# Two groups per scan in a Mamba layer: moving the decay factors from PSUM to SBUF, with smaller edits around it and in the last layer

## The chip, the core and the metric

The kernel runs on one core of a Trainium2 chip. A core has five engines with an instruction queue each: TensorE (PE) for matrix products, VectorE (DVE), ScalarE (ACT) and GpSimd (POOL) for elementwise work, and SyncE (SP), which here issues the DMA transfers. Operands lie in SBUF or, for results of PE, in the eight banks of PSUM. POOL here works on SBUF only. The metric is the device time of the whole kernel in microseconds (us): a single launch that computes all four layers. Before the change it is 8328.65 us, the median of three runs (8322.74 to 8329.06).

## The reference

The input is four images of 56 x 56 positions with 128 channels, in fp32. Four layers follow, each added to its input: a neighbourhood attention, a Mamba block, an additive attention with a mixture of 64 experts, and a full attention with 8 experts of which each token takes two. The change touches the second and the last.

The Mamba layer runs two passes over 224 sequences (4 images x 56 rows) of 56 steps. In each, 256 inner channels have 16 states each:

```python
delta = jax.nn.softplus(dt @ dtw + dtb)
A = -jnp.exp(A_log)
deltaA  = exp(delta[.., d] * A[d, n])           # decay of a state
deltaBu = delta[.., d] * u[.., d] * Bm[.., n]   # its input
h = deltaA * h + deltaBu                        # along the 56 steps
y = sum over n of h * Cm[.., n];   y = y + u * Dp
```

The last layer's experts work on a layer norm of the tokens, x:

```python
router_probs = softmax(x @ router_w + router_b)     # 8 experts
top_p, top_i = top_k(router_probs, 2);  top_p = top_p / sum(top_p)
expert_out = einsum('bnd,edc->bnec', x, expert_w) + expert_b
out = sum over the two of top_p * expert_out
```

## The kernel before, in words

The kernel works through the layers one after the other. Within a layer the order of instructions on PE, ACT, DVE and POOL is written out by hand: each engine runs its own instructions in the order in which the Python code emits them, and waits at an instruction until what it needs is there.

**Layer 1 (Mamba), `layer1`.** Tokens are cut into 28 chunks of 448 (8 sequences of 56). A chunk and one of the two passes make a block; there are 56 blocks (`order`). A block's 256 x 16 states are taken 128 at a time as 32 groups: 8 channels with 16 states each fill the 128 partitions, and the 448 tokens lie along the row. Two groups are a pair, so a block has 16 pairs (`PAIRS`) and the layer 896 (`n_pairs`). For each pair p the main loop emits:

- `select(p + 1)`: PE spreads delta times A over the 128 states (matrix "A_pick", tile "a", L650) and delta times u (matrix "pick", tile "u", L657), two matmuls each of 32 input rows. ACT turns "a" into the decay exp(a), in place, in PSUM (L660). "a" has two buffers of two banks, "u" one of two banks, "y" and the general tile "m" one bank each: PSUM is full.
- `scan(p)`: DVE runs the recurrence along the row, one scan for each of the two groups (L672). At a sequence's first step delta is set to 1e30, so that the decay is 0 and the scan starts afresh. POOL multiplies the result by C (tile "bc", L676), in place.
- `sums(p - 5)`, at every second pair: PE adds the 16 states of a channel into "y" (L682). The states "hs" have seven buffers.
- `inputs(p + 1)`: DVE multiplies "u" by B into "dBu", one product for each group (L667).

Around the pairs, `first` and `last` place the other steps of a block at fixed pairs. `mamba_pre` prepares the next block during the present one: a convolution by PE ("raw"), silu on ACT, a projection, spreads of delta, B and C by PE (L808), the softplus, whose maximum with 0 is on DVE (`parts`, L818) and whose last three steps are on POOL (L834, L837, L840), and "du" = delta times u in two halves of 64 partitions each on POOL (L846), with rows exchanged so that the four matmuls of a pair lie on four different sets of 32 rows. `gate` (L697, DVE), `project` (PE) and `pass_on` finish a block.

**Layer 3, `layer3`.** For each image and chunk of 448 queries, 25 key tiles are worked off as units: `weights` makes scores "q" on PE (L1548) and their exponent on ACT, `weighted` adds up "o" on PE (L1559), which has a single bank. Other steps stand at fixed units in `at`: `prepare_chunk` of the next image, `experts_chunk` of the last chunk (copy of "o", L1533 and L1534, then the return to tokens, and `token_choice`: a layer norm, the router with its bias added by DVE, the choice of two, the biases of the experts by a transposed gate and a matmul, L1706 to L1720, then the experts themselves, L1726 and L1731). During the first chunks the experts of layer 2 for the last image run between these units, with a PSUM bank of their own ("h").

**Layer 0** matters for reading the profile: its weights "e" are multiplied by a table (L428), three heads on DVE and one on POOL, with all operands in SBUF.

Of the kernel before, what the change touches and what calls it, by code (L numbers as in the profile page):

```python
# [10 lines left out]
AF = mybir.ActivationFunctionType  # L11
ALU = mybir.AluOpType
# [7 lines left out]
P = 128  # L20
# [17 lines left out]
PAIRS = DI // 16  # L38
LONG = 1.0e30

AH = 16
# [63 lines left out]
class Hybrid:  # L105
# [485 lines left out]
    def layer1(self):  # L591
# [5 lines left out]
        with ExitStack() as ctx:  # L597
# [20 lines left out]
            h = {}  # L618
            pre, yg, A, U, V, HS, py = {}, {}, {}, {}, {}, {}, {}

# [15 lines left out]
            def place(p):  # L636

                j, i = divmod(p, PAIRS)
                return j, i // 8, i // 2 % 4, i % 2 * 2

            def select(p):
                if p >= n_pairs:
                    return
                j, f, q, r0 = place(p)
                l = order[j][2]
                A[p] = self.t(ps_a, [P, 2, 512], "a")[:, :, :CH]
                U[p] = self.t(ps_u, [P, 2, 512], "u")[:, :, :CH]
                for k in range(2):
                    own = slice((r0 + k) * HD, (r0 + k + 1) * HD)
                    nc.tensor.matmul(  # L650
                        A[p][:, k], w["A"][own, l, f, q, :], pre[j]["delta"][own, f],
                        start=True, stop=True,
                    )
                for k in range(2):
                    r = (r0 + k + 2) % 4
                    own = slice(r * HD, (r + 1) * HD)
                    nc.tensor.matmul(  # L657
                        U[p][:, k], w["pick"][own, q, :], pre[j]["du"][own, f], start=True, stop=True
                    )
                nc.scalar.activation(A[p], A[p], AF.Exp)  # L660

            def inputs(p):
                if p < n_pairs:
                    V[p] = self.t(sm, [P, 2, CH], "dBu")
                    u = U.pop(p)
                    for k in range(2):
                        nc.vector.tensor_mul(V[p][:, k], u[:, k], pre[p // PAIRS]["bc"][:, 0])  # L667

            def scan(p):
                HS[p] = self.t(sm, [P, 2, CH], "hs", bufs=7)  # L670
                for k in range(2):
                    nc.vector.tensor_tensor_scan(  # L672
                        HS[p][:, k], A[p][:, k], V[p][:, k], 0.0, op0=ALU.mult, op1=ALU.add
                    )
                bc = pre[p // PAIRS]["bc"]
                nc.gpsimd.tensor_mul(HS[p], HS[p], bc[:, 1:2].to_broadcast([P, 2, CH]))  # L676
# [76 lines left out]
            for p in range(-PAIRS - 2, n_pairs + PAIRS):  # L753
                for step in first.get(p, []):
                    step()
                if p >= -1:
                    select(p + 1)
                if 0 <= p < n_pairs:
                    scan(p)
                if p % 2 and 0 <= p - 5 < n_pairs:  # L760
                    sums(p - 5)
                for step in last.get(p, []):
                    step()
                if p >= -1:
                    inputs(p + 1)

    def mamba_pre(self, pre, j, block, h, w, sm, m):
# [44 lines left out]
        def parts(i):  # L812
            if i == 0:
                r["e"] = self.t(sm, [P, NHALF, CH], "sp_e", bufs=1)
                r["delta"] = self.t(sm, [P, NHALF, CH], "delta")
            dtb = w["dtb"][:, l, i : i + 1]
            nc.scalar.activation(r["e"][:, i], ps[0], AF.Abs, bias=dtb)
            nc.vector.tensor_scalar(r["delta"][:, i], ps[0], dtb, 0.0, op0=ALU.add, op1=ALU.max)  # L818

# [21 lines left out]

        def du(k):
            if k == 0:
                r["du"] = self.t(sm, [P, NHALF, CH], "du")
            to, of = slice(k * 64, k * 64 + 64), slice(64 - k * 64, 128 - k * 64)
            nc.gpsimd.tensor_mul(r["du"][to], r["delta"][of], r["us"][of])  # L846
            if k == 1:

                for f in range(NHALF):
                    nc.gpsimd.memset(seqs(r["delta"][:, f])[:, :, 0:1], LONG)  # L850

# [7 lines left out]
        def resed(f):  # L859
# [11 lines left out]
            (6, spread, 2), (7, low), (7, spread, 3), (8, log1p), (9, delta), (9, res, 0),  # L871
            (10, du, 0), (10, res, 1), (11, du, 1), (PAIRS + 2, silu, "raw_res", "sres"),
        ]
# [588 lines left out]
    def layer3(self):  # L1462
# [6 lines left out]
        with ExitStack() as ctx:  # L1469
            wp = ctx.enter_context(tc.tile_pool(name="l3_w", bufs=1))  # L1470
            w = {}
            w["rw"] = self.load(wp, [P, E3], "rw", a["L3_ffn_router_w"])
            w["rb"] = self.load(wp, [TP, E3], "rb", a["L3_ffn_router_b"].partition_broadcast(TP))
            w["ew"] = self.load(wp, [P, E3, C], "ew", a["L3_ffn_expert_w"].rearrange("e d c -> d e c"))
            w["eb"] = self.load(wp, [E3, C], "eb", a["L3_ffn_expert_b"])
            shift = self.t(wp, [P, 1], "shift")
# [9 lines left out]
            ps_m = ctx.enter_context(tc.tile_pool(name="l3_m", bufs=2, space=PSUM))  # L1486
            ps_h = ctx.enter_context(tc.tile_pool(name="l3_h", bufs=1, space=PSUM))
            ps_e = ctx.enter_context(tc.tile_pool(name="l3_e", bufs=2, space=PSUM))
            ctx.enter_context(
                tc.manual_schedule(engines={ET.PE, ET.Activation, ET.DVE, ET.Pool})  # L1490
# [64 lines left out]
            def weighted(b, c, t):  # L1555
                if t == 0:
                    po[b, c] = self.t(ps_o, [P, 512], "o")[:, :CH]
                n = tiles[t][1]
                nc.tensor.matmul(  # L1559
                    po[b, c], xk[b][:n, t, :], es.pop((b, c, t))[:n], start=(t == 0), stop=(t == N - 1)  # L1560
                )
# [26 lines left out]
            for steps, num in ((chosen, 4), (passed, 2)):  # L1588
                for n, step in enumerate(steps):
                    at.setdefault(u // den, []).append(step)  # L1590
                    u += 0 if step.holds else num
            assert u // den < 2 * NCH * N + 6
            for u in range(max(at) + 3):
                if u < len(units):
                    weights(*units[u])
                if 0 <= u - 2 < len(units):
                    weighted(*units[u - 2])
                for step in at.get(u - 2, []):
                    step()
# [8 lines left out]

    def normed_chunk(self, b, c, sm, m, eps, turned):

# [21 lines left out]
        def norm():  # L1632
            r["xa"] = self.t(sm, [TP, TC, C], "lc_xa", bufs=4)
            for k in range(TC):
                nc.vector.tensor_scalar(
                    r["xa"][:, k, :], x[:, TC * c + k, :], r["mv"][:, k, 0:1], r["r"][:, k : k + 1],
                    op0=ALU.subtract, op1=ALU.mult,
                )

        def turn():  # L1640
# [10 lines left out]
    def token_choice(self, b, c, w, sm, m, ps_e):  # L1651
# [11 lines left out]
        def route():  # L1663
            ps = m()
            for k in range(TC):
                nc.tensor.matmul(
                    ps[:TP, k * E3 : (k + 1) * E3], r["xT"][:, k * TP : (k + 1) * TP], w["rw"],
                    start=True, stop=True,
                )


            r["pr"] = pr = tile4("r_pr", 2 * E3 - K3)
            nc.gpsimd.memset(pr[:, :, E3:], NOTHING)
            r["p8"] = p8 = pr[:, :, 0:E3]
            nc.vector.tensor_tensor(
                p8, ps[:TP, : TC * E3].rearrange("p (t e) -> p t e", e=E3),
                w["rb"].unsqueeze(1).to_broadcast([TP, TC, E3]), op=ALU.add,
            )
            r["red"] = red = self.t(sm, [TP, TC], "r_red")
            nc.vector.tensor_reduce(red, p8, axis=AX.X, op=ALU.max)  # L1680
            nc.vector.tensor_tensor(p8, p8, per_token(red), op=ALU.subtract)

# [19 lines left out]

        def turn_gate():
            r["pg"] = pg = m()
            for k in range(TC):
                nc.tensor.transpose(  # L1706
                    pg[:E3, k * TP : (k + 1) * TP], r["gate"][:, k, :], self.ident[:TP, :TP]
                )

        def turned_gate():  # L1710
            r["gT"] = self.t(sm, [E3, CH], "gT")
            nc.scalar.copy(r["gT"], r["pg"][:E3, :CH])

        def biases():
            pb = m().rearrange("p (k c) -> p k c", c=C)
            for k in range(TC):
                nc.tensor.matmul(
                    pb[:TP, k, :], r["gT"][:, k * TP : (k + 1) * TP], w["eb"], start=True, stop=True
                )
            nc.vector.tensor_add(x4, pb[:TP], x4)  # L1720

        def experts(k):
# [13 lines left out]
        def store():  # L1736
# [4 lines left out]
        return (  # L1741
            self.normed_chunk(b, c, sm, m, w["eps"], turned)
            + [(10, route), (12, exp), (13, choose), (18, turn_gate), (19, turned_gate), (21, biases)]
            + [(21 + 2 * k, bind(experts, k)) for k in range(TC)] + [(21 + 2 * TC, store)]
# [44 lines left out]
```

## Time and profile before

| what | value |
|---|---|
| median of three runs | 8328.65 us |
| the profiled execution | 8338.93 us, its span 8337.2 us |
| busy PE, DVE, ACT, POOL | 84%, 75%, 61%, 35% of the span |
| Mamba (645 to 3825 us of the span) | 3180 us, 56 blocks |
| layer 3 (from 6720 us) | 1617 us |
| granted clock of PE in the span | 0.924 |

The profile page and the trace come from the same execution. In a line of groups there stand the source line, the engine, the operation, output and inputs by the program's names, the shapes and the count; then the total busy time in us and the mean of one in ns; then the idle time of the engine just before these instructions, and who ended most of it. [...] consecutive instructions can overlap a little in the records, and an instruction that has been started and then has to wait inside the engine shows a longer time.

### The profile page before, as it was taken

What the parts mean: (1) busy time and instruction counts of PE and PEld (TensorE: products, weight loads), DVE (VectorE), ACT (ScalarE), POOL (GpSimd) and SP (SyncE); (2) the same over time, 40 slices, a digit from 0 to 9 for tenths busy, and PEclk for the clock granted to TensorE, in tenths of its full rate; (3) what the DMA queues carried; (4) which work ended last, traced back from release to release, by engine and by line L of the source; (5) the groups of instructions that cost most, each with busy time, mean ns of one, the idle gap of its engine ahead of it and who ended that gap; (6) DMA issues with size and microseconds to landing.
All of it is one profiled execution on the core that took longest, in us unless ns stands there. A gap on an engine that the chain in (4) does not pass through costs nothing.

```text
span 8337.2 us, 109252 instructions
## 1 busy us (share of the span) xinstructions
PE 7035.0 (84%) x41373; PEld 2773.9 (33%) x41373; DVE 6274.1 (75%) x12303; ACT 5125.5 (61%) x5001; POOL 2902.1 (35%) x1997
## 2 busy tenths in 40 slices
PE   8878998999899999996777777777777889999998
PEld 4432333333333332332222222222222344454444
DVE  6768998999898899897777878777787754344434
ACT  4445555555455555554998799889889964333332
POOL 4537876877677768772000000000001000000000
PEclk9988998999898889897999999999999989999999
DMA  2000000000000000000000000000003101210000
GB/s 51 1 13 1 1 1 1 1 1 1 1 1 1 1 1 1 1 1 5 1 1 1 5 1 1 1 5 1 1 25 113 44 4 54 86 44 5 5 5 6
DMA packets 84469, 102.05 MB, mean 12 GB/s; under 512 B 21132, under 2 KB 49700, under 8 KB 83236
## 3 DMA queue, kind: packets, MB, share of 16 engines
q1 hardware_dynamic: 83941, 95.06, 3.8%
q8 instruction: 327, 5.36, 0.3%
q14 instruction: 201, 1.64, 0.1%
HBM read 84.76 MB, written 10.29 MB: 11 GB/s over the span
## 4 chain that ended last, share of the span: by engine, by line
PE 48%; ACT 21%; DVE 20%; issue 9%; POOL 1%; SPq 0%; ACTq 0%; DMA 0%; DVEq 0%; POOLq 0%
ACT th L1021 12%; DVE hs L672 7%; PE q L1548 6%; PE o L1559 6%; PE a L650 6%; PE s L1032 5%; PE m L779 5%; DVE th L1012 5%; PE y L682 3%; PE o L1059 2%; PE pe L1726 2%; PE u L657 2%; DVE e L428 2%; DVE dBu L667 2%; PE m L808 1%
## 5 line engine op out<-in xcount | busy, mean ns | idle before, releaser
L1021 ACT ACTIVATE th<-th 128x3136 f32<-128x3136 f32 (+12 forms) x1120 | 2293.3, 2094 | 217.6 <-DVE th L1012 169.2
L1012 DVE TENSOR_SCALAR th<-fT,g 128x784 f32<-128x784 f32 (+6 forms) x3920 | 1934.3, 561 | 468.2 <-PE s L1032 440.5
L676 POOL TENSOR_TENSOR hs<-hs,bc 128x896 f32<-128x896 f32 x896 | 1859.0, 2084 | 688.8 <-DVE hs L672 578.3
L1032 PE MATMUL s<-th,place 128*32 128x392 f32 (+7 forms) x14336 | 1487.7, 491 | 714.5 <-ACT th L1021 711.1
L672 DVE TENSOR_TENSOR_SCAN hs<-a,dBu 128x448 f32<-128x448 f32 x1792 | 1845.1, 1070 | 160.8 <-POOL hs L676 87.4
L660 ACT ACTIVATE a<-a 128x896 f32<-128x896 f32 x896 | 808.5, 902 | 931.2 <-PE u L657 431.0
L650 PE MATMUL a<-delta,A_pick 32*128 32x448 f32 x3584 | 1080.3, 638 | 97.0 <-DVE hs L672 93.1
L657 PE MATMUL u<-du,pick 32*128 32x448 f32 x3584 | 1033.8, 656 | 26.7 <-DVE dBu L667 22.6
L667 DVE TENSOR_TENSOR dBu<-u,bc 128x448 f32<-128x448 f32 x1792 | 1014.1, 606 | 45.8 <-PE u L657 40.8
L1032 PEld LDWEIGHTS s<-th,place 128*32 128x32 f32 (+1 forms) x14336 | 423.0, 111 | 1648.8 <-ACT th L1021 1130.5
L1553 ACT ACTIVATE e<-q,shift 128x448 f32<-128x448 f32 (+1 forms) x700 | 443.0, 634 | 774.3 <-PE q L1548 774.0
L1559 PE MATMUL o<-e,xk 128*128 128x448 f32 (+1 forms) x1400 | 657.3, 551 | 61.4 <-ACT oT L1534 61.4
L1548 PE MATMUL q<-xT 128*128 128x448 f32 (+1 forms) x1400 | 656.1, 551 | 7.7 <-ACT e L1553 7.7
L1050 POOL TENSOR_TENSOR e<-e,later 112x112 f32<-112x112 f32 x112 | 79.6, 710 | 1589.8 <-ACT e L1043 961.9
L650 PEld LDWEIGHTS a<-delta,A_pick 32*128 32x128 f32 x3584 | 338.3, 202 | 706.8 <-issue 327.5
L682 PE MATMUL y<-hs,sum 128*32 128x448 f32 x3584 | 494.4, 626 | 3.6 <-POOL hs L676 3.6
L1731 DVE SCALAR_TENSOR_TENSOR X<-pe,r_gate,X 112x128 f32<-112x128 f32 x896 | 313.8, 350 | 188.9 <-PE pe L1726 153.4
L1059 PE MATMUL o<-e,xa 112*128 112x392 f32 (+5 forms) x1024 | 418.5, 531 | 1.1 <-POOL e L1050 1.1
L657 PEld LDWEIGHTS u<-du,pick 32*128 32x128 f32 x3584 | 299.5, 204 | 297.4 <-DVE dBu L667 294.5
L1559 PEld LDWEIGHTS o<-e,xk 128*128 128x128 f32 (+1 forms) x1400 | 262.0, 192 | 351.8 <-issue 273.5
L1548 PEld LDWEIGHTS q<-xT 128*128 128x128 f32 (+1 forms) x1400 | 248.8, 189 | 235.4 <-issue 218.7
L1522 POOL MEMSET xk<- 128x4 f32 (+1 forms) x28 | 2.9, 105 | 847.0 <-DVE xk L1521 701.2
(263 smaller groups left out, 7959.4 us busy)
## 6 DMA issues: line engine op xcount, KB each, us to landing
wide<-in_L_ffn_weight SPq DMA_DIRECT2D x64, 1024.0 KB
X<-in_x SPq DMA_DIRECT2D x8, 784.0 KB
out<-X SPq DMA_DIRECT2D x28, 224.0 KB
M<-wide SPq DMA_DIRECT2D x4, 784.0 KB
wide<-M SPq DMA_DIRECT2D x4, 784.0 KB
e_edge<-dtab SPq DMA_DIRECT2D x42, 49.0 KB
cw<-in_L_conv_conv_w SPq DMA_DIRECT2D x1, 1024.0 KB
c_h<-in_L_ffn_weight SPq DMA_DIRECT2D x16, 64.0 KB
```

Source lines behind the costliest of these rows:

```text
L650: nc.tensor.matmul(A[p][:, k], w["A"][own, l, f, q, :], pre[j]["delta"][own, f], start=True, stop=True,)
L657: nc.tensor.matmul(U[p][:, k], w["pick"][own, q, :], pre[j]["du"][own, f], start=True, stop=True)
L660: nc.scalar.activation(A[p], A[p], AF.Exp)
L667: nc.vector.tensor_mul(V[p][:, k], u[:, k], pre[p // PAIRS]["bc"][:, 0])
L672: nc.vector.tensor_tensor_scan(HS[p][:, k], A[p][:, k], V[p][:, k], 0.0, op0=ALU.mult, op1=ALU.add)
L676: nc.gpsimd.tensor_mul(HS[p], HS[p], bc[:, 1:2].to_broadcast([P, 2, CH]))
L682: nc.tensor.matmul(py[j, f][r * HD : (r + 1) * HD, :], w["sum"][:, q, :], HS[p + r // 2][:, r % 2], start=False, stop=(q == QG - 1),)
L1012: nc.vector.tensor_scalar(th[i][:, blk, lo:hi], fT[j][:, lo:hi], im[order[j][0]]["g"][:, at : at + 1], None, op0=ALU.add,)
L1021: nc.scalar.activation(own, own, AF.Tanh)
L1032: nc.tensor.matmul(ps[j, J][QW * blk : QW * blk + rows, h, lo:hi], place[:, off : off + rows], z[:, blk, h * HALF + lo : h * HALF + hi], s ...
L1548: nc.tensor.matmul(ps[:n, :CH], xT[b][:, k : k + n], xT[b][:, c * CH : (c + 1) * CH], start=True, stop=True,)
L1559: nc.tensor.matmul(po[b, c], xk[b][:n, t, :], es.pop((b, c, t))[:n], start=(t == 0), stop=(t == N - 1))
```

## The change

*In Mamba:*

- `select(p)` selects the decay of pair p and the input "u" of pair p + 1, so that the loop makes inputs two pairs ahead of the scan (`inputs(p + 2)`, "dBu" with three buffers).
- ACT writes the exponent to a new tile "E" in SBUF, two groups side by side in a row of 896, instead of in place in PSUM.
- one scan of 896 elements takes the place of two of 448; one product "dBu" of 896 the place of two.
- for pairs 1, 4 and 15 of each 16 (`BY_POOL`), ACT copies "u" to SBUF and POOL makes "dBu".
- the maximum with 0 in the softplus is a Relu on ACT.
- "du" is one POOL operation over 128 partitions; the exchange of rows is gone, since "a" and "u" of one loop step now belong to two pairs, which lie on different rows.

*In layer 3:*

- A layer norm's output sums to zero over the channels, so the last channel can be left out: the last weight row is subtracted from all rows of the router and expert weights, and its place is taken by the bias; the last channel of the normed tokens is set to 1 (POOL). This needs two more loads, two subtractions on DVE and two small DMAs at the start of the layer. The router's bias addition and the transposed gate with its matmuls, copy and addition go.
- When the experts of layer 2 are done, their PSUM bank becomes a second bank for "o".

```diff
+BY_POOL = (1, 4, 15)
...
             def select(p):
...
-                nc.scalar.activation(A[p], A[p], AF.Exp)
+                if 0 <= p < n_pairs:
+                    E[p] = self.t(sm, [P, 2 * CH], "E")
+                    nc.scalar.activation(halves(E[p]), A.pop(p), AF.Exp)
+                if p + 1 < n_pairs and (p + 1) % PAIRS in BY_POOL:
+                    V[p + 1] = self.t(sm, [P, 2 * CH], "dBu", bufs=3)
+                    v = halves(V[p + 1])
+                    nc.scalar.copy(v, U.pop(p + 1))
+                    nc.gpsimd.tensor_mul(v, v, pre[j]["bc"][:, 0:1].to_broadcast([P, 2, CH]))
 
             def inputs(p):
-                if p < n_pairs:
-                    V[p] = self.t(sm, [P, 2, CH], "dBu")
-                    u = U.pop(p)
-                    for k in range(2):
-                        nc.vector.tensor_mul(V[p][:, k], u[:, k], pre[p // PAIRS]["bc"][:, 0])
+                if p in U:
+                    V[p] = self.t(sm, [P, 2 * CH], "dBu", bufs=3)
+                    nc.vector.tensor_mul(
+                        halves(V[p]), U.pop(p), pre[p // PAIRS]["bc"][:, 0:1].to_broadcast([P, 2, CH])
+                    )
 
             def scan(p):
-                HS[p] = self.t(sm, [P, 2, CH], "hs", bufs=7)
-                for k in range(2):
-                    nc.vector.tensor_tensor_scan(
-                        HS[p][:, k], A[p][:, k], V[p][:, k], 0.0, op0=ALU.mult, op1=ALU.add
-                    )
+                flat = self.t(sm, [P, 2 * CH], "hs", bufs=7)
+                nc.vector.tensor_tensor_scan(
+                    flat, E.pop(p), V.pop(p), 0.0, op0=ALU.mult, op1=ALU.add
+                )
+                HS[p] = halves(flat)
...
-                if p >= -1:
+                if p >= -2:
                     select(p + 1)
...
-                if p >= -1:
-                    inputs(p + 1)
+                inputs(p + 2)
...
-            nc.vector.tensor_scalar(r["delta"][:, i], ps[0], dtb, 0.0, op0=ALU.add, op1=ALU.max)
+            nc.scalar.activation(r["delta"][:, i], ps[0], AF.Relu, bias=dtb)
...
-            to, of = slice(k * 64, k * 64 + 64), slice(64 - k * 64, 128 - k * 64)
-            nc.gpsimd.tensor_mul(r["du"][to], r["delta"][of], r["us"][of])
+            nc.gpsimd.tensor_mul(r["du"], r["delta"], r["us"])
...
+                last = self.load(
+                    tp, [P, E3, C], "ew_last", a["L3_ffn_expert_w"][:, C - 1, :].partition_broadcast(P)
+                )
+                nc.vector.tensor_sub(w["ew"], w["ew"], last)
+                rlast = self.load(
+                    tp, [P, E3], "rw_last", a["L3_ffn_router_w"][C - 1, :].partition_broadcast(P)
+                )
+                nc.vector.tensor_sub(w["rw"], w["rw"], rlast)
+            nc.sync.dma_start(out=w["ew"][C - 1 : C, :, :], in_=a["L3_ffn_expert_b"].unsqueeze(0))
+            nc.sync.dma_start(out=w["rw"][C - 1 : C, :], in_=a["L3_ffn_router_b"].unsqueeze(0))
...
-                    po[b, c] = self.t(ps_o, [P, 512], "o")[:, :CH]
+                    po[b, c] = self.t(sums[c % len(sums)], [P, 512], "o")[:, :CH]
...
+            def passed_by():
+                spare.close()
+                sums.append(spare.enter_context(tc.tile_pool(name="l3_o2", bufs=1, space=PSUM)))
...
+            if ones:
+                nc.gpsimd.memset(r["xa"][:, :, C - 1 : C], 1.0)
...
-        def turn_gate():
...
-        def turned_gate():
...
-        def biases():
...
-            nc.vector.tensor_add(x4, pb[:TP], x4)
```

## The prediction

> **What bounds the kernel now.** I read the stages first, then the groups of the stage that changes most, then single instructions. The table by stage (us; then busy time and instruction count of PE, its weight load, DVE, ACT, POOL; clock, DMA share, GB/s), cut at layer 0, Mamba, layer 2, layer 3:
>
> ```profile
> 0.00:645.00 645.00, 516.79 (x5768) 281.38 (x5768) 442.23 (x577) 299.50 (x412) 294.94 (x285) 0.90 0.10 21
> 645.00:3825.00 3180.00, 2904.65 (x13364) 978.99 (x13364) 2914.24 (x3909) 1696.11 (x2002) 2423.87 (x1311) 0.90 0.00 1
> 6720.00:8337.00 1617.00, 1504.36 (x5205) 758.07 (x5204) 702.53 (x2817) 584.23 (x1024) 35.29 (x169) 0.97 0.09 27
> ```
>
> Mamba is 3180 us, 56 blocks of 56.8 us, with DVE busy 92% of it, PE 91% and POOL 76%. Layer 3 is PE's. The costliest groups of Mamba (page, part 5):
>
> ```profile
> L676 POOL TENSOR_TENSOR hs<-hs,bc 128x896 f32<-128x896 f32 x896 | 1859.0, 2084 | 688.8 <-DVE hs L672 578.3
> ...
> L672 DVE TENSOR_TENSOR_SCAN hs<-a,dBu 128x448 f32<-128x448 f32 x1792 | 1845.1, 1070 | 160.8 <-POOL hs L676 87.4
> ...
> L667 DVE TENSOR_TENSOR dBu<-u,bc 128x448 f32<-128x448 f32 x1792 | 1014.1, 606 | 45.8 <-PE u L657 40.8
> ```
>
> Per pair DVE does two scans and two products, POOL one product. In a quiet stretch (timeline: start, length) DVE is the pace, 3.02 us a pair, and POOL's operations lie beside the scans without lengthening them:
>
> ```profile
> 1533.50 2.06 DVE L672 TENSOR_TENSOR_SCAN hs<-a,dBu 128x448 f32<-128x448 f32 x2
> 1535.48 1.13 DVE L667 TENSOR_TENSOR dBu<-u,bc 128x448 f32<-128x448 f32 x2
> 1536.52 2.06 DVE L672 TENSOR_TENSOR_SCAN hs<-a,dBu 128x448 f32<-128x448 f32 x2
> ```
>
> Here the scan reads "a" in PSUM and only "dBu" in SBUF. What happens when DVE has both inputs in SBUF, layer 0 shows (source line 428, same product split between DVE and POOL; ns min/median/max). Started together at 104.4 us:
>
> ```profile
> L428 DVE TENSOR_TENSOR e<-e,e_inner x2: 1146/1265/1384, 104.4 to 105.7; 112x1176 f32<-112x1176 f32 x1, 112x168 f32<-112x168 f32 x1
> L428 POOL TENSOR_TENSOR e<-e,e_inner x2: 391/1309/2227, 104.4 to 106.6; 112x392 f32<-112x392 f32 x1, 112x56 f32<-112x56 f32 x1
> ```
>
> The same shapes at 124.0 us (DVE) and 122.3 us (POOL), where the other engine ran nothing of the kind:
>
> ```profile
> L428 DVE TENSOR_TENSOR e<-e,e_inner x2: 325/850/1376, 124.0 to 125.3; 112x1176 f32<-112x1176 f32 x1, 112x168 f32<-112x168 f32 x1
> L428 POOL TENSOR_TENSOR e<-e,e_inner x2: 304/656/1009, 122.3 to 123.3; 112x392 f32<-112x392 f32 x1, 112x56 f32<-112x56 f32 x1
> ```
>
> Alone, POOL's 392 elements take 1.009 us; beside DVE's 1176 they take 2.227: they wait 1.22 us, that whole operation. Then DVE's 168 elements take 1.146 instead of 0.325 us: they wait 0.82 us for POOL. The two take turns, whole instructions at a time. POOL's turn was 0.82/392 = 2.1 ns per element, so 1.88 us for 896.
>
> [...] no row of this trace shows a scan with two SBUF inputs. [...] 1.00 us from one 448-element scan to the next against 0.51 for a product. That leaves one scan of 896 elements near 1.93 us (two take 1.98, less one fixed part of some 0.05).
>
> **The change, part by part.**
>
> *Mamba, DVE.* Per block of 16 pairs: 32 scans become 16 of 1.93 (31.7 to 30.9 us); 32 products become 13 of about 1.04 (16.6 to 13.5); two maxima of 0.68 go to ACT (1.4 to 0). Gates and additions stay, 1.7. DVE's own work falls from 51.4 to 46 us a block.
>
> *Mamba, POOL.* The 16 products on "hs" stay, 2.09 each; three "dBu" products come (6.3); "du" becomes one operation instead of two half-partition ones that cost 2.075 each (-2.1). With three of the softplus: 16+3+1+3 = 23 operations, 48 us. Its memsets, 0.1 each, read nothing.
>
> *Mamba, ACT.* Three copies of U by 0.93, two Relu by 0.63: +4 us on 30. Covered by more than 20 us of idle time a block; POOL's "dBu" queues behind the copy, and the scan that needs it comes two pairs later.
>
> *Mamba, PE.* Same matmuls, U one pair earlier. The exponent now goes to E in SBUF, so A's bank is free after the exponent instead of after the scan: the waits of L650 on the scan (93 us in all) go. PE at 52 us a block isn't what sets the end below.
>
> [...] E in SBUF is also the price. The scan now has two SBUF inputs, and all 23 POOL operations read SBUF. Scan and POOL must take turns, and the pair's own chain is scan, then POOL's product on its result. Per pair: scan 1.93 + 0.15 until POOL starts (end at 1506.41, POOL at 1506.55) + POOL's turn 1.88 = 3.96; the next scan follows. DVE's product (PSUM and SBUF) fits under POOL's turn. Sixteen pairs: 63.4. The seven other POOL operations take turns too, 7 x 2.0 = 14.0. Sum 77.4; I add 1 for the stalls at table loads (DVE idled about 5 a block before, but POOL's queue now fills most of it): 78.5 us a block. Lower end: POOL always has something waiting, so hand-overs vanish: 16 x (1.87 + 1.88) + 7 x 1.9 = 73.3. Upper end: the scan waits for POOL's recorded end, 2.08: 16 x 4.16 + 7 x 2.1 = 81.3, with 3 of stalls 84. [...] What is late next is PE's sums (they wait for POOL), and behind them in PE's queue A and U of later pairs; PE and ACT have 25 and 44 us of slack a block, so it ends there.
>
> 56 x 78.5 = 4396, against 3180: +1216 (from +925 to +1524).
>
> *Layer 3.* Gone per chunk: four transposes of the gate and eight passes of bias matmuls. On PE, at 8132.14 to 8132.62 and 8137.67 to 8138.72, they take 0.48 + 1.05 and disturb neighbours by about 0.4: 1.9 x 28 = -53. The second bank removes the wait of the first "o" of a chunk on the copy of the last:
>
> ```profile
> L1559 PE MATMUL o<-e,xk 128*128 128x448 f32 (+1 forms) x1400 | 657.3, 551 | 61.4 <-ACT oT L1534 61.4
> ```
>
> 2.3 us a chunk, but only once the last image's experts are through (last addition of L1435 at 7440.7), so 16 of 28 chunks: -37. Last chunk's chain, without cover: -4 (transposes, copy, matmuls, 0.69 addition). Start: DVE's subtraction waits for two 512 KB loads where the first statistics ran at 6729.4 with none, and these queue behind it; the one load of before came within some 5 us of its issue, so with the 1.1 us of subtraction +9. On SP the two bias rows wait for the subtractions and "back" behind them; it is needed only 70 us later. POOL's memset of ones lies between norm and turn, which are three units apart: nothing. Sum -85 (-40 to -110). Layers 0 and 2 are untouched.
>
> Total: profiled execution 8338.9 (span 8337.2) + 1216 - 85 = 9470; the median of the runs is 10 lower, so 9460.
>
> **Rivals.**
>
> *No turns for the scan (ends faster).* [...] Then POOL's 48.4 and DVE's 46 set the pace; with some 3.5 of stalls 52 a block, 2912: -268 - 85, so 7976 (7850 to 8150). It decides if at least 20 us of a block's 78.5 overlap, 1.27 us per pair.
>
> *Shared by cycles (ends slower).* [...] 23 x 1.88 + 16 x 0.93 = 58, with stalls 60, 3360: +180 - 85, so 8424. Against: layer 0's waits are whole instructions.
>
> *The change doesn't do what it says.* The scan stays in order behind late inputs: not plausible, inputs come two pairs ahead.
>
> **How the numbers follow.** Turns 0.82: 9460, own range 9200 to 9800. Shared 0.04. No turns 0.14. Faster 0.14, same (within 0.2%, about what a measurement here can tell) 0.01, slower 0.85. The range 9150 to 9820 takes the first case with both bounds and a margin; about 0.2 stays outside, nearly all of it the rivals.
>
> **What would show it.** Right: the scan's mean far above 1.93 us (recorded with its wait, near 2.9 or more), or POOL's product above 2.08, or both, summing to about 3.9 a pair; DVE's products on "u" unchanged; Mamba near 4400 us; PE's clock up. The scan near 1.95 and POOL near 2.08 overlapping would prove me wrong at once. In layer 3 the chunk pitch should fall by about 2 us before 7440 (of the old time) and 4 after it.

## The result: 11% slower, and the profile after

The changed kernel takes 9277.42 us (median of four runs, 9276.63 to 9281.59), the kernel before 8325.69 us on the same chip (8322.29 to 8329.06): a ratio of 1.1144, with a 95% interval of 1.1125 to 1.1163. The forecast was 9460 us, with a range of 9150 to 9820.

The table by stage of the changed kernel, with the columns of before, Mamba and layer 3:

```profile
648.00:4842.00 4194.00, 3405.12 (x13362) 1133.05 (x13360) 3504.35 (x1839) 1890.29 (x2280) 4111.45 (x1425) 0.77 0.00 1
7700.00:9280.00 1580.00, 1490.42 (x5150) 736.63 (x5150) 705.36 (x2838) 600.24 (x1028) 41.07 (x203) 0.96 0.09 28
```

From the start of the first scan to the end of the last, Mamba grew from 3178 to 4189 us (+1010). From there to the end of the span, 4511 became 4440 us (-71): layer 3 became 75 us shorter, and layer 2, which the change doesn't touch, took 4 us longer. POOL, with three more products a block, is now recorded as busy for 98% of Mamba. The costliest groups on the page of the changed kernel say what that busy time is (after the bar: busy time, mean ns of one; then the idle time before it and what ended most of it):

```profile
L684 DVE TENSOR_TENSOR_SCAN hs<-E,dBu 128x896 f32<-128x896 f32 x896 | 2700.2, 3022 | 438.1 <-POOL dBu L672 232.5
L689 POOL TENSOR_TENSOR hs<-hs,bc 128x896 f32<-128x896 f32 x896 | 2814.4, 3163 | 17.5 <-DVE hs L684 17.5
...
L677 DVE TENSOR_TENSOR dBu<-u,bc 128x896 f32<-128x896 f32 x728 | 774.9, 1064 | 219.9 <-PE u L661 217.1
```

The scan's mean is 3.02 us, and POOL's product went from 2.08 to 3.16 us on the same operands. DVE's product, with one input in PSUM, is as fast as expected (1.06 us). Two timelines of the same stretch (start, length, and in brackets the idle time before and what ended it) show how. First DVE:

```profile
1506.99 2.02 DVE L684 TENSOR_TENSOR_SCAN hs<-E,dBu 128x896 f32<-128x896 f32 x1 [2.82 <-ACT E L667]
1508.93 1.06 DVE L677 TENSOR_TENSOR dBu<-u,bc 128x896 f32<-128x896 f32 x1
1509.91 2.86 DVE L684 TENSOR_TENSOR_SCAN hs<-E,dBu 128x896 f32<-128x896 f32 x1
1512.69 1.06 DVE L677 TENSOR_TENSOR dBu<-u,bc 128x896 f32<-128x896 f32 x1
1513.68 2.86 DVE L684 TENSOR_TENSOR_SCAN hs<-E,dBu 128x896 f32<-128x896 f32 x1
1516.46 1.06 DVE L677 TENSOR_TENSOR dBu<-u,bc 128x896 f32<-128x896 f32 x1
```

Then POOL:

```profile
1507.87 3.02 POOL L846 TENSOR_TENSOR sp_e<-sp_e,sp_w 128x896 f32<-128x896 f32 x1 [0.76 <-ACT sp_w L845]
1510.85 3.80 POOL L689 TENSOR_TENSOR hs<-hs,bc 128x896 f32<-128x896 f32 x1
1514.62 3.79 POOL L849 TENSOR_TENSOR sp_ln<-sp_ln,sp_e 128x896 f32<-128x896 f32 x1
```

The scan that starts at 1509.91 ends at 1512.77. Less the 2.02 us that the scan before it (at 1506.99) was recorded with, it got going only at about 1510.75, when POOL's "sp_e" was nearly through (POOL's next operation starts at 1510.85). POOL's product, started at 1510.85, waits for that end inside its own record, so that 3.80 us stand where 1.88 are left after that end (1512.77 to 1514.65). The next scan, started at 1513.68, waits for it. A scan and a POOL operation together take 3.77 us (1509.91 to 1513.68), twice 1.88. Over a whole block the median is 74.6 us for 16 scans and 23 POOL operations: 39 turns of 1.913 us.

### The profile page after: what moved, and what is told of

The parts are those of the page before. It is cut to its first block, busy times and chain, and to the rows that moved or that the text cites. A ratio compares the mean times of both kernels' runs of the same rounds, so it can differ in the third digit from the quotient of the medians.

```text
span 9279.8 us, 106976 instructions
## 1 busy us (share of the span) xinstructions
PE 7500.2 (81%) x41037; PEld 2894.1 (31%) x41037; DVE 6840.5 (74%) x10177; ACT 5306.4 (57%) x5253; POOL 4589.1 (49%) x2137
## 4 chain that ended last, share of the span: by engine, by line
PE 29%; POOL 21%; issue 19%; ACT 17%; DVE 12%; SPq 0%; DMA 0%; ACTq 0%; DVEq 0%; POOLq 0%
POOL hs L689 12%; ACT th L1030 11%; PE q L1572 6%; PE o L1583 6%; PE s L1041 5%; DVE th L1021 4%; POOL dBu L672 4%; DVE hs L684 2%; PE o L1068 2%; PE pe L1737 2%; POOL sp_ln L849 2%; POOL delta L852 2%; DVE e L430 2%; POOL du L856 1%; PE u L661 1%
## 5 line engine op out<-in xcount | busy, mean ns | idle before, releaser
L684 DVE TENSOR_TENSOR_SCAN hs<-E,dBu 128x896 f32<-128x896 f32 x896 | 2700.2, 3022 | 438.1 <-POOL dBu L672 232.5
L689 POOL TENSOR_TENSOR hs<-hs,bc 128x896 f32<-128x896 f32 x896 | 2814.4, 3163 | 17.5 <-DVE hs L684 17.5
L661 PE MATMUL u<-du,pick 32*128 32x448 f32 x3584 | 1229.7, 753 | 580.6 <-DVE dBu L677 421.1
L667 ACT ACTIVATE E<-a 128x896 f32<-128x896 f32 x896 | 821.9, 917 | 1374.2 <-PE u L661 836.0
L652 PE MATMUL a<-delta,A_pick 32*128 32x448 f32 x3584 | 1225.3, 699 | 0.0
L677 DVE TENSOR_TENSOR dBu<-u,bc 128x896 f32<-128x896 f32 x728 | 774.9, 1064 | 219.9 <-PE u L661 217.1
L661 PEld LDWEIGHTS u<-du,pick 32*128 32x128 f32 x3584 | 359.0, 234 | 959.2 <-DVE dBu L677 691.1
L695 PE MATMUL y<-hs,sum 128*32 128x448 f32 x3584 | 571.9, 716 | 5.9 <-POOL hs L689 5.9
L652 PEld LDWEIGHTS a<-delta,A_pick 32*128 32x128 f32 x3584 | 389.4, 224 | 600.7 <-issue 475.1
L672 POOL TENSOR_TENSOR dBu<-dBu,bc 128x896 f32<-128x896 f32 x168 | 541.4, 3223 | 50.3 <-ACT dBu L671 50.3
```

The costliest lines, as they stand in the source:

```text
L652: nc.tensor.matmul(A[p][:, k], w["A"][own, order[j][2], f, q, :], pre[j]["delta"][own, f], start=True, stop=True,)
L661: nc.tensor.matmul(U[p + 1][:, k], w["pick"][own, q, :], pre[j]["du"][own, f], start=True, stop=True,)
L667: nc.scalar.activation(halves(E[p]), A.pop(p), AF.Exp)
L672: nc.gpsimd.tensor_mul(v, v, pre[j]["bc"][:, 0:1].to_broadcast([P, 2, CH]))
L677: nc.vector.tensor_mul(halves(V[p]), U.pop(p), pre[p // PAIRS]["bc"][:, 0:1].to_broadcast([P, 2, CH]))
L684: nc.vector.tensor_tensor_scan(flat, E.pop(p), V.pop(p), 0.0, op0=ALU.mult, op1=ALU.add)
```

## Experiments

Every comparison below is with the kernel before, run on the same chip. "Turns" is the theory that a scan with two SBUF inputs and a POOL operation that reads SBUF exclude each other. A block's time is the median distance of every sixteenth pair's first scan; "Mamba" is measured from the first scan to the end of the last.

### One edit on the kernel before: the decay to SBUF

```diff
-                nc.scalar.activation(A[p], A[p], AF.Exp)
+                E[p] = self.t(sm, [P, 2, CH], "E")
+                nc.scalar.activation(E[p], A.pop(p), AF.Exp)
...
-                        HS[p][:, k], A[p][:, k], V[p][:, k], 0.0, op0=ALU.mult, op1=ALU.add
+                        HS[p][:, k], E[p][:, k], V[p][:, k], 0.0, op0=ALU.mult, op1=ALU.add
```

> The kernel before with one edit: ACT writes the decay to a new tile in SBUF and the two scans of 448 read it there. [...] 16 pairs of scans plus 21 POOL operations of 896 elements are 37 turns a block of about 1.91 us, 70.8 us a block against 56.8, so Mamba about 3960 us and the kernel about 9110 us (8950 to 9250); scans and POOL products both recorded far above 1.07 and 2.08 us. Rival, the load on POOL (its three extra products make it late): no change here, 8326 us. Rival, the scan itself is slower with two SBUF inputs: scans longer, but POOL's products stay at 2.08 us.

Measured: 9502.49 us, ratio 1.1397 (1.1380 to 1.1414); 77.4 us a block. This edit alone costs more than the whole change. POOL has nothing more to do than before, so the load on POOL is out as the cause. The size was missed, and one of the two expected lengthenings isn't there. From the groups of this kernel's page:

```profile
L673 DVE TENSOR_TENSOR_SCAN hs<-E,dBu 128x448 f32<-128x448 f32 x1792 | 3150.5, 1797 | 0.1
L677 POOL TENSOR_TENSOR hs<-hs,bc 128x896 f32<-128x896 f32 x896 | 1863.6, 2080 | 1695.0 <-DVE hs L673 1574.7
```

The scans grew from 1.07 to 1.80 us, POOL's product stayed at 2.08. Read with the rival's eyes, this is a slow scan and no contention. The timelines correct that reading (in brackets the idle time before the instruction and who ended it):

```profile
1520.82 2.09 POOL L677 TENSOR_TENSOR hs<-hs,bc 128x896 f32<-128x896 f32 x1 [2.10 <-DVE hs L673]
1521.62 3.22 DVE L673 TENSOR_TENSOR_SCAN hs<-E,dBu 128x448 f32<-128x448 f32 x2
1525.00 2.08 POOL L677 TENSOR_TENSOR hs<-hs,bc 128x896 f32<-128x896 f32 x1 [2.10 <-DVE hs L673]
```

POOL works 2.08 us and then waits 2.10 us for the next pair of scans; in that time two scans fit at their old speed, and indeed three in ten scans are still recorded at 1.06 us. It is a strict chain, scan then product, 4.18 us a pair: 16 x 4.18 + 5 x 2.08 = 77.3, close to the measured block. Nearly all waiting is in DVE's records.

### The same with one scan for a pair

```diff
-                V[p] = self.t(sm, [P, 2, CH], "dBu")
+                V[p] = self.t(sm, [P, 2 * CH], "dBu")
...
-                for k in range(2):
-                    nc.vector.tensor_tensor_scan(
-                        HS[p][:, k], E[p][:, k], V[p][:, k], 0.0, op0=ALU.mult, op1=ALU.add
-                    )
+                flat = self.t(sm, [P, 2 * CH], "hs", bufs=7)
+                nc.vector.tensor_tensor_scan(flat, E[p], V[p], 0.0, op0=ALU.mult, op1=ALU.add)
+                HS[p] = flat.rearrange("p (k q) -> p k q", k=2)
```

> The kernel with the decay in SBUF (e_sbuf), the two scans of a pair made one of 896. The 9502 us of e_sbuf were more than turns alone give (77.4 us a block against 37 turns of 1.913 = 70.8). If the split is why (POOL slips in between two scans, catches up, and then waits for the next scan [...]): about 70.8 us a block, 9120 us (9000 to 9250), and POOL's product recorded well above 2.08 us. If the inputs made only one pair ahead are why: 9450 us or more, POOL's product at 2.08.

Measured: 9223.59 us, ratio 1.1061 (1.1044 to 1.1077); 71.7 us a block. As expected: with one scan the order of turns changes, and POOL's product is now recorded with its wait, in the groups of this kernel's page:

```profile
L677 POOL TENSOR_TENSOR hs<-hs,bc 128x896 f32<-128x896 f32 x896 | 2662.1, 2990 | 445.6 <-DVE hs L674 427.1
...
L674 DVE TENSOR_TENSOR_SCAN hs<-E,dBu 128x896 f32<-128x896 f32 x896 | 2344.2, 2616 | 94.7 <-ACT bc L824 1.0
```

Once POOL is one operation behind, its next one is already started and waiting when a scan ends (2.99 us in its record, against 2.08 in the kernel before), and the hand-over costs little: 37 turns of 1.94 us fill the block. With two scans of 448 POOL caught up. The trace of that kernel shows it, where POOL has another operation to do:

```profile
1525.80 5.05 DVE L673 TENSOR_TENSOR_SCAN hs<-E,dBu 128x448 f32<-128x448 f32 x2
1527.03 2.87 POOL L835 TENSOR_TENSOR sp_e<-sp_e,sp_w 128x896 f32<-128x896 f32 x1
```

The first of the two scans ends at 1528.03. POOL's operation then runs to 1529.90, and the second scan, started at 1527.95, ends only at 1530.85. POOL has slipped in between the two scans and is free again before the pair's product can start.

### The decay in SBUF, but the other input in PSUM

The decay stays in SBUF; the second input leaves it.

```diff
-                    V[p] = self.t(sm, [P, 2, CH], "dBu")
-                    u = U.pop(p)
+                    V[p] = u = U.pop(p)
...
-            ps_a = ctx.enter_context(tc.tile_pool(name="l1_a", bufs=2, space=PSUM))
-            ps_u = ctx.enter_context(tc.tile_pool(name="l1_u", bufs=1, space=PSUM))
+            ps_a = ctx.enter_context(tc.tile_pool(name="l1_a", bufs=1, space=PSUM))
+            ps_u = ctx.enter_context(tc.tile_pool(name="l1_u", bufs=2, space=PSUM))
```

> The kernel with the decay in SBUF (e_sbuf) with one more edit: the input product dBu is written in place in PSUM (two buffers for u, one for a), so that the scan reads the decay in SBUF and dBu in PSUM, one SBUF input. Turns: the contention goes although the decay stays in SBUF: scans 1.06 to 1.1 us, POOL's product 2.08 us, a block near 55 us, the kernel about 8330 us (8200 to 8420). Rival, a decay in SBUF is what costs (its write by ACT, or the scan's reading): 9400 us or more, as before this edit.

Measured: 8492.35 us, ratio 1.0186 (1.0169 to 1.0203), against 1.1397 without this edit. The groups of its page:

```profile
L676 POOL TENSOR_TENSOR hs<-hs,bc 128x896 f32<-128x896 f32 x896 | 1866.9, 2086 | 892.6 <-DVE hs L672 778.2
...
L672 DVE TENSOR_TENSOR_SCAN hs<-E,u 128x448 f32<-128x448 f32 x1792 | 1847.4, 1072 | 96.7 <-DVE u L667 2.4
```

Scan and product are back at 1.07 and 2.09 us with the decay still in SBUF. So it is the second SBUF input, not the decay's new place, that brings the turns. The time missed its range upward:

```profile
1515.92 1.27 DVE L667 TENSOR_TENSOR u<-u,bc 128x448 f32<-128x448 f32 x2
1517.33 2.06 DVE L672 TENSOR_TENSOR_SCAN hs<-E,u 128x448 f32<-128x448 f32 x2
```

The two products now take 1.27 us from start to end instead of 1.13, and the scan that reads them starts 1.41 us after their start instead of 1.04; DVE's quiet pace is 3.39 us a pair instead of 3.02.

### The changed kernel with the decay in PSUM

The two groups are written to the end of one bank and the start of the next, so that one scan can read them as a row of 896.

```diff
-                    A[p] = self.t(ps_a, [P, 2, 512], "a")[:, :, :CH]
+                    A[p] = self.t(ps_a, [P, 1024], "a")[:, 512 - CH : 512 + CH]
...
-                    E[p] = self.t(sm, [P, 2 * CH], "E")
-                    nc.scalar.activation(halves(E[p]), A.pop(p), AF.Exp)
+                    E[p] = A.pop(p)
+                    nc.scalar.activation(E[p], E[p], AF.Exp)
```

> The changed kernel with the decay back in PSUM: the two groups of a pair are written next to each other across the border of two banks, the exponent is in place, and one scan of 896 reads it there; all else of the change stays. Turns: the contention goes, scan near 1.98 us and POOL's product at 2.08 us, a block is paced by POOL's 23 operations and DVE's 46 us with stalls, about 52 us, so the kernel at about 7990 us (7850 to 8150). Rival, the load on POOL or the other edits are what costs: it stays above 8700 us. Rival, a slow scan: as with turns, but POOL's product was then not waiting in the changed kernel.

Measured: 8345.33 us, ratio 1.0017 (1.0010 to 1.0024). The groups of its page:

```profile
L684 DVE TENSOR_TENSOR_SCAN hs<-a,dBu 128x896 f32<-128x896 f32 x896 | 1806.4, 2017 | 468.1 <-ACT a L667 458.0
...
L689 POOL TENSOR_TENSOR hs<-hs,bc 128x896 f32<-128x896 f32 x896 | 1853.7, 2083 | 271.4 <-DVE hs L684 180.3
```

The contention is gone, and with it 932 of the 952 us that the change had cost. So nearly all of its loss is this one thing; Mamba is still 71 us longer than before, which the gain in layer 3 covers. But the gain that I had worked out for a kernel without turns isn't there: Mamba took 3249 us, not 2912, because DVE now waits 458 us for the exponent. The next runs look for that gain.

### Fewer turns: no input product on POOL

```diff
-BY_POOL = (1, 4, 15)
+BY_POOL = ()
```

On the changed kernel:

> The changed kernel with no input product on POOL (all 16 of a block on DVE, no copies on ACT). Turns: [...] 36 x 1.913 = 68.9 us a block instead of 74.6, -321 us in all, so about 8955 us (8880 to 9050), although DVE has 3.2 us a block more to do. Rival, DVE with a slow scan is the pace: slower than the changed kernel, about 9450 us. Rival, only POOL's late products are the cost: back to 8300 us or below.

Measured: 8967.73 us, ratio 1.0758 (1.0741 to 1.0774); 68.4 us a block against the 68.9 of 36 turns. Giving work from a POOL that was recorded as busy for 98% of Mamba to a DVE that has more work already makes the kernel 3% faster, because the turns fill the block (36 of 1.90 us) and neither engine's own work does. If a slow scan had been the limit, the kernel would have become slower.

On the kernel with the decay in PSUM:

> The changed kernel with the decay in PSUM (a_psum) and no input product on POOL. In a_psum the contention was gone, but Mamba took 3249 us because DVE waited 458 us for ACT's exponent. If the copies of u on ACT and POOL's products at three pairs cause these waits: a block is DVE's 48.5 us and some 4 of stalls, 52.5, so Mamba 2950 to 3050 us and the kernel about 8090 us (8000 to 8200). If one scan that holds both banks to its end is the cause (a's two buffers come free later): 8300 us or more.

Measured: 8288.17 us, ratio 0.9942 (0.9928 to 0.9957); Mamba 3206 us. The three products on POOL and their copies cost some 60 us there, not 250; the time lies between the two forecasts, close to the second. The waits before the scan did fall, from 468 to 269 us:

```profile
L684 DVE TENSOR_TENSOR_SCAN hs<-a,dBu 128x896 f32<-128x896 f32 x896 | 1803.2, 2013 | 269.0 <-issue 163.7
```

But DVE now has the three products to do, and its busy time in Mamba rose from 2599 to 2750 us, which uses up most of that.

### Where the gain without turns went

Three theories for the missing gain were tried: the order of the matmuls on PE, DVE's own work, and an exponent that comes too late. None brought it back. First, that "a" and "u" run one after the other on PE. Before, they cover 1.69 us of PE a pair, where the four matmuls side by side take 1.02. The edit puts the matmuls of "u" ahead of those of "a" in `select`, once on the kernel of the last run above and once on the kernel before with the layer 3 edits. The first of the two:

```diff
+                if p + 1 < n_pairs:
+                    j, f, q, r0 = place(p + 1)
+                    U[p + 1] = self.t(ps_u, [P, 2, 512], "u")[:, :, :CH]
...
                 if 0 <= p < n_pairs:
                     j, f, q, r0 = place(p)
                     A[p] = self.t(ps_a, [P, 1024], "a")[:, 512 - CH : 512 + CH]
...
-                if p + 1 < n_pairs:
-                    j, f, q, r0 = place(p + 1)
-                    U[p + 1] = self.t(ps_u, [P, 2, 512], "u")[:, :, :CH]
```

> a_psum_none (decay in PSUM, one scan, no input product on POOL) with the two matmuls of u put ahead of those of a in each loop step. In a_psum_none the contention is gone but Mamba takes 3206 us: a (freed by the scan) and u (freed by the product 1.07 us later) run one after the other on PE, 1.64 us of PE a pair where four matmuls side by side take 1.02. If this serial pair is the limit: with u first PE waits once and runs all four together, a block falls from 55.7 to about 52 us, the kernel to about 8100 us (8030 to 8200). If PE's time isn't the limit, or the exponent now comes too late for the scan: 8288 us or more.

> The kernel before with the layer 3 edits and, in each loop step of Mamba, the matmuls of u ahead of those of a. If the serial pair on PE limits the kernel before too: less than 8255 us, about 8180 (8100 to 8240). If DVE's 3.02 us a pair is the limit (91.6% busy): 8255 us within 20, or more where the exponent comes too late for the scan.

Measured: 8280.52 us (ratio 0.9941, 0.9925 to 0.9958), the same as without, and 8325.49 us (0.9990, 0.9981 to 0.9998) for the other order on the kernel before, 70 us worse than with the layer 3 edits alone. PE's busy time fell from 6978 to 6659 us in the first, the time didn't: PE's own work is not the limit. What is left is seen on ACT in the first of these kernels. Its timeline (start, length):

```profile
1533.73 1.28 ACT L842 ACT_TABLE_LOAD   x1
1535.02 0.95 ACT L842 ACTIVATE sp_ln<-sp_w 128x896 f32<-128x896 f32 x1
1535.88 0.51 ACT L835 COPY bc<-m 128x448 f32<-128x448 f32 x1
1536.41 1.28 ACT L667 ACT_TABLE_LOAD   x1
1537.70 0.90 ACT L667 ACTIVATE a<-a 128x896 f32<-128x896 f32 x1
```

DVE in the same stretch (in brackets its idle time before the instruction):

```profile
1534.49 1.07 DVE L677 TENSOR_TENSOR dBu<-u,bc 128x896 f32<-128x896 f32 x1
1538.69 2.02 DVE L684 TENSOR_TENSOR_SCAN hs<-a,dBu 128x896 f32<-128x896 f32 x1 [3.13 <-issue]
```

The exponent of a pair stands behind the logarithm of the next block's softplus and two table loads of 1.28 us, one for the logarithm and one for the exponent after it, and the scan waits 3.13 us. In the kernel before, such a wait was 1.35 us in the same part of a block. Over the whole of Mamba the waits before the scan are 271 us in this kernel and 161 in the kernel before. The other two theories were tried on another layout, with the decay in SBUF and dBu in PSUM, which leaves one SBUF input: first that layout with one scan and the layer 3 edits, then with the maximum on ACT (less work for DVE), then with the decay a pair further ahead, behind the matmuls of "u", and "du" in one operation as in the change. The last two steps (the edit of "du" isn't shown):

```diff
-            nc.vector.tensor_scalar(r["delta"][:, i], ps[0], dtb, 0.0, op0=ALU.add, op1=ALU.max)
+            nc.scalar.activation(r["delta"][:, i], ps[0], AF.Relu, bias=dtb)
```

```diff
-                A[p] = self.t(ps_a, [P, 2, 512], "a")[:, :, :CH]
                 U[p] = self.t(ps_u, [P, 1024], "u")[:, 512 - CH : 512 + CH]
...
-                E[p] = self.t(sm, [P, 2 * CH], "E")
+                p += 1
+                if 0 <= p < n_pairs:
+                    a = self.t(ps_a, [P, 2, 512], "a")[:, :, :CH]
...
+                    E[p] = self.t(sm, [P, 2 * CH], "E", bufs=3)
...
-                if p >= -1:
+                if p >= -2:
                     select(p + 1)
```

> The decay in SBUF, dBu in place in PSUM across two banks, one scan and one product of 896, and the layer 3 edits; nothing on POOL that was not there before. No turns: DVE 16 x 2.95 + 2.9 = 50.1 us a block, with 3 to 5 of stalls 54, Mamba about 3020 us, layer 3 -75: about 8100 us (8000 to 8230), faster than both kernels. If dBu in PSUM makes u late (its two buffers are held until the scan): above 8255 us.

> v_psum_one_l3 with one more part of the change, the maximum of the softplus as a Relu on ACT. DVE loses 112 operations of 0.68 us. If DVE's own work is the limit there: up to 76 us less, about 8200 us (8190 to 8240). If what the scan waits for is the chain on ACT (exponents behind table loads), which gets 112 operations of 0.63 us more: 8270 us or more.

> v_relu with the decay made one pair further ahead (a of pair p + 2 in each loop step, E with three buffers; du in one operation as in the change). One SBUF input, so no turns. If the scans' waits for ACT at the start of each block are the limit that is left: 3 us a block less, about 8080 us (8000 to 8180), the fastest so far. If not: within 40 us of v_relu.

Measured: 8269.22 us (ratio 0.9917, 0.9903 to 0.9932), 8272.95 us (0.9931, 0.9915 to 0.9948) and 8315.74 us (0.9984, 0.9977 to 0.9991). The first missed its range. Moving 76 us of DVE's work to ACT, the second, gained nothing; the scan's waits for ACT grew instead, from 36 to 132 us (without and with the step):

```profile
L673 DVE TENSOR_TENSOR_SCAN hs<-E,u 128x896 f32<-128x896 f32 x896 | 1808.9, 2019 | 141.8 <-ACT E L661 36.1
L673 DVE TENSOR_TENSOR_SCAN hs<-E,u 128x896 f32<-128x896 f32 x896 | 1810.3, 2020 | 248.4 <-ACT E L661 131.8
```

With the exponent ahead, the third, these waits are gone from the list of DVE's waits, but waits for PE have come, and the kernel is 43 us slower than the second, where at most 40 were expected if the exponent wasn't the limit. From the list of waits of the last kernel, DVE in Mamba alone (us in total, times, longest):

```profile
DVE X L732 <- PE m L716: 120.0, 26, 4.9
DVE u L669 <- PE a L658: 98.1, 65, 4.1
DVE u L669 <- PE u L647: 44.6, 51, 2.2
```

Mamba took 3184, 3182 and 3220 us in the three. A part of the missing gain in these three is DVE's own pace: the scan starts 1.20 us after the product that writes to PSUM, against 0.98 with the decay in PSUM and dBu in SBUF, so that a quiet pair takes 3.14 us where I had counted 2.95, and 16 pairs fill 50 of a block's 57 us. The kernels with the decay in PSUM have a quiet pace of 2.91 us and wait more. Why both come out near 3180 to 3200 us is left open; PE's order, ACT's chain and DVE's work seem to lie so close together that taking away one of them shows the next, but that is not shown. No run had a Mamba stage clearly faster than that of the kernel before.

### Layer 3 alone

The kernel before with the edits in `layer3`, `normed_chunk` and `token_choice`.

> The kernel before with the layer 3 edits alone. From the two traces layer 3 falls by 68 us (start +10, first eleven chunks -10, the other sixteen -63, tail -5): 8258 us (8245 to 8275). Rival, it depends on what Mamba leaves behind (clock of PE): less than 40 us gained.

Measured: 8255.35 us, ratio 0.9904 (0.9888 to 0.9921). This is the fastest kernel of the study, 77 us below the kernel before, which took 8331.84 us on that chip, and inside its forecast. The "start +10" of the expectation was not layer 3's, though: it held 3.5 us by which the first scan came later and 4 us of layer 2. Layer 3's own start, from its first statistics to the first matmul on "o", lost 3 us, and layer 3 as a whole gained 75. The kernel differs from the changed kernel by the whole of the Mamba edits. The accumulation of "o" shows the second bank in the groups of this kernel's page (61.4 us of waiting before):

```profile
L1574 PE MATMUL o<-e,xk 128*128 128x448 f32 (+1 forms) x1400 | 656.0, 551 | 29.3 <-ACT oT L1549 29.3
```

## Why the prediction was right, by its own steps

**What bounds, and the turns: right.** The step that the forecast hung on, from tensor_tensor in layer 0 to the scan, was an estimate of mine, since no trace of before showed a scan with two SBUF inputs. It held: the edit that gives the scan two SBUF inputs costs 14% by itself, and taking either input back to PSUM ends the contention (scans of 448 at 1.07 us, one of 896 at 2.02, POOL's product at 2.08 to 2.09). POOL's turn of 1.88 us for 896 elements, worked out from a 392-element operation, is close to what the alternation shows (3.77 us for a scan and a POOL operation; less 1.93 for the scan, 1.84).

**The sum for Mamba: a size was off.** 78.5 us a block were forecast, 74.6 measured, +1216 against +1010 us. Mis-sized was the term for hand-over and chain: the centre was a chain, with 0.15 us after each scan until POOL starts, 2.0 for each extra operation and 1 us of stalls, and the lower end, 73.3, turns that follow each other without a gap. It is nearly the second: 39 x 1.913 = 74.6. The three extra POOL products aren't needed for that: without them the 36 turns take 1.90 us each. The strict chain exists too, in the kernel with split scans (77.4 us, 4.18 a pair; the upper end had 4.16). That the total fell inside the range is hardly a matter of errors that cancel: the forecast for Mamba was 206 us too high, and the gain forecast for layer 3 was too large by 10.

**The signs: one was wrong.** The scan's mean was to be near 2.9 us or more (it is 3.02) and POOL's product above 2.08 (3.16), as they are. But the two were to sum to about 3.9 us a pair, and the means sum to 6.18: each of the two records holds the wait for the other. It is the distance between starts, 3.77 us, that shows the sum.

**Pricing of the parts: mixed.** The single scan: 1.93 estimated, the 1.98 of two less about 0.05. The 0.05 agrees with layer 0, where 1176 elements alone took 1.376 us and 168 took 0.325: at those 1.04 ns an element 448 take 0.47 of the 0.51 us of a product. The records with no contention give 2.02, of which the next DVE operation overlaps 0.09. DVE's product: 1.04 estimated, 0.98 to 1.01 from start to start. That the copies and Relu on ACT cost nothing fits the changed kernel, where the turns are the limit, but wasn't tested there; without turns the copies and POOL products cost some 60 us.

**Layer 3: -85 forecast, -75 measured.** From its first statistics to the end of the span it took 1608 us before and 1533 after. By the starts of the chunks: the first chunk is unchanged, the eleven after it, beside the experts, gained 9.7 us (I had 1.9 each, 21), the sixteen after them 62.7 (3.9 each; I had 4.2), the tail 5.2 (4), and the start lost 3.0 (9): DVE idled 2.17 us for the second load and subtracted for 1.23. Off were the price of the start and the assumption that PE's saved time counts fully while the experts of layer 2 run between the units; it counted for half, and why wasn't tested.

**"PE's clock up": wrong.** In Mamba it fell from 0.90 to 0.77. It cost nothing that can be told from these runs, since PE, busy for 81% of Mamba then, wasn't the limit.

**The rivals.** "No turns" fell, and its own number would have failed too: 7976 us was worked out for a kernel with no contention, and the kernel in which the contention is gone, with the decay in PSUM, takes 8345. I had allowed 3.5 us of stalls a block; without turns, the waits for ACT alone were 458 us over 56 blocks, 8.2 us a block. "Shared by cycles" fell: the turns are whole instructions here too, 1.93 us for the scan and 1.84 for POOL's operation in the 3.77 between starts, and a block takes 74.6 us, not 60. That a scan would claim only 0.93 us beside POOL was an estimate of mine that no run shows.

## What to carry to other kernels

Before moving an operand from PSUM to SBUF, count the SBUF inputs of the DVE instructions that will read it, and what POOL does at that moment. Here one input in PSUM was enough to let both engines run undisturbed (scan 1.07 us, POOL's product 2.09, with the decay still in SBUF). Two SBUF inputs made them take turns, 3.77 us for a scan of 896 and a POOL operation, and two engines that had been busy for 92% and 76% of Mamba shared one sequence of turns. In the profile both engines looked busy (84% and 98%) and their operations slow (3.02 and 3.16 us); the test is whether the same operation on the same operands has two durations, and whether starts alternate. When several engines are nearly full, as here without turns (DVE 92% and PE 91% of Mamba before), price the waits that come next before counting on a faster engine: 76 us taken off DVE gained nothing, the scan's waits for ACT grew by 96.

## What the runs showed of the hardware beyond that

- The wait for a turn stood inside the record of whichever instruction came second: almost on DVE alone (scans at 1.80 us, POOL's product at 2.08), or on both (3.02 and 3.16), with the same exclusion underneath.
- A DVE scan and an ACT exponent ran over one row of 896 that crosses the border of two PSUM banks, at 2.02 and 0.90 us.
- The scan started later when the DVE product that it reads was written to PSUM: from the start of two products of 448 to the start of the scan it took 1.41 us, against 1.04 with the product in SBUF; with one product of 896, 1.20 against 0.98.
- PE's granted clock in Mamba was 0.90 before, 0.87 with the decay in PSUM and no product on POOL, 0.77 after the change, 0.74 in the kernel with split scans on SBUF. PE's idle time alone doesn't decide it: with the matmuls of "u" first on the kernel before, PE was busy for 2520 of Mamba's 3238 us at 0.91, and with the decay in PSUM and no product on POOL for 2889 of 3207 at 0.87. What does wasn't tested.
